# Adjacency tiles kept in bf16 in 32 buffers, layer 1's sums dealt anew to the steps, and a new order of the end

## The chip, the core and the metric

The kernel runs on one core of a Trainium2 chip. The metric is the device time of one execution in microseconds (us). Three runs of the kernel before took 260.06, 260.49 and 262.83 us, median 260.49. One more execution was profiled: 261.3 us, of which 259.5 us lie between its first and last instruction (the span). All times from a trace are counted from the span's start.

Engines: PE is TensorE (matrix products), DVE VectorE, ACT ScalarE, POOL GpSimd, SP SyncE. POOL and SP also issue transfers (DMA). Each engine works through its own queue in order; semaphores make one wait for another.

## The reference

Two layers of a graph network over N = 4096 nodes with 64 features; `adj` is 4096 x 4096 of zeros and ones, one in 256 is set.

```python
def layer0(x, adj, weight, bias):
    support = x @ weight
    mask = (adj != 0)
    rank = cumsum(mask, axis=1); deg = rank[:, -1:]
    k = minimum(deg, 100); pos = rank - (deg - k)
    w = mask * where(pos > 0, 0.5 ** (k - pos), 0)
    return w @ support + bias

def layer1(X, adj, W, b):
    deg = clip(sum(adj, axis=1) + 1, 1)
    h = (adj @ X + X) / deg
    z = relu(concat([X, h]) @ W + b)
    return z / maximum(norm(z), 1e-12)

x = layernorm(x + layer0(x, adj, weight, bias))
x = layernorm(x + layer1(x, adj, W, b))
```

Layer 0 weighs each neighbour by its rank counted from the row's end, so every row has to be counted from the right. Layer 1 needs layer 0's output for all neighbours. Both read the whole of `adj`.

## The kernel before

**Tiles.** The nodes (rows of `adj`, columns of its transpose) are cut into 8 slabs g of 512, the neighbours into 8 blocks k of 512 (each four times 128). A tile (g, k) of the transposed `adj` is read from HBM as float32 (1 MB) and written to SBUF as bf16 (512 KB) by a transfer that POOL issues (`load_next`, L106). There are 64 tiles, and 64 **steps**, one for each tile: slab by slab, in each slab from block 7 down to block 0. Step i handles tile i.

**A step** (loop from L542) does, on PE: `count` (column sums of tiles ahead, L247), `weigh` (ranks by two sets of 16 small products, L277 and L286), `some_sums` (a **group**, that is four products of layer 1's sum over one tile, L313), at the end of a chunk `spread` (L265), and `gather` (layer 0's sum with the weights of the step before, L304). ACT and DVE each turn half of the ranks into weights (L293, L294). The chunks are 1 to 4 tiles long (4 in slabs 4 to 7); the counts of the next chunk are made two tiles at a time in every second step, so step s of a pair counts tiles s+4 and s+5 where chunks are 4 long, and all of the next four in step 30. PE's queue is in order, so a count that waits for its tile's landing holds up all that follows.

**Loads.** Six are issued ahead; step i issues load i+6. The pool `a16` has 23 buffers; a load takes one that is free in program order or waits until its last reader is done. A tile's last reader is its group of layer 1's sum. For slabs 0 to 3, blocks 7 to 4, `keep_next` makes an fp8 copy of a tile (zeros and ones are exact in it) in two halves, one a step, three in four on ACT (L329) and the others on DVE (L327), so that the bf16 buffer comes free without a sum.

**Layer 1's sums.** A group (g, k) can only be summed when layer 0 is done for the nodes of block k, which is some steps after slab k's last step (`ready`: i >= 8(k+1) + 7, and tile (g, k) is there). `jobs` lists (slab, first block, end block); each job accumulates in one PSUM bank (`acc1`) and is then added to the slab's `part` by `evict_part`, on DVE. 27 of the 64 groups are done within the steps, 37 after them.

**Layer 0's epilogue** of slab g runs some steps later (`first_hT` ... `first_c1`, hung to steps by `at`): layer norm, the split of x1 into two fp16 halves (`x1hl`), and the products for layer 1 (`c1`).

**The end** (from L737): the last gather, slab 7's epilogue, the remaining groups (`own`, and `own_half` for slab 7 in two halves of its columns), and layer 1's epilogue by **units** of one or two slabs: `last_hT` (PSUM plus part to SBUF), `last_pz` (product with the neighbour weights), `last_z`, `last_sq`, `last_ss` (row norms), `last_rn` (1/sqrt by POOL's power or by a root of ACT and four steps of DVE), `last_y` (and the added x1, by POOL or DVE), `last_mv` (moments), `last_r`, `last_o`, `store`. The order is written by hand: units (5,2), (0,1), (4,3), 6, 7. Its tiles come from pools of two buffers each.

Of the kernel before, what the change touches and what calls it, by code (L numbers as in the profile page):

```python
# [12 lines left out]
F8 = mybir.dt.float8e4  # L13
# [23 lines left out]
KEPT = 4  # L37
# [3 lines left out]
def adj_resnorm_kernel(  # L41
# [31 lines left out]
    a16p = ctx.enter_context(tc.tile_pool(name="a16", bufs=23))  # L73
    a8p = ctx.enter_context(tc.tile_pool(name="a8", bufs=KEPT * (NK - KEPT)))
# [3 lines left out]
    small = ctx.enter_context(tc.tile_pool(name="small", bufs=2))  # L78
# [236 lines left out]

    to_keep = [(g, k, h) for g in range(KEPT) for k in range(NK - 1, KEPT - 1, -1) for h in range(2)]
    kept = {}

    def keep_next(i):
        if not to_keep:  # L320
            return
        g, k, h = to_keep.pop(0)
        if h == 0:
            kept[g, k] = a8p.tile([P, KB, R], F8, tag="a8", name=f"a8_{g}_{k}")
        qs = slice(h * KB // 2, (h + 1) * KB // 2)
        if i % 4 == 3:
            nc.vector.tensor_copy(kept[g, k][:, qs, :], A[g][k][:, qs, :], saturate=False)  # L327
        else:
            nc.scalar.copy(kept[g, k][:, qs, :], A[g][k][:, qs, :], saturate=False)  # L329
        if h == 1:  # L330
            A[g][k] = kept[g, k]


    jobs = [(0, 0, 2), (1, 0, 2), (2, 0, 2), (3, 0, 3), (2, 2, 4), (0, 2, 4), (1, 2, 4)]
    jobs += [(4, 0, 4), (5, 0, 5), (6, 0, 3)]
    have = {g: 0 for g in range(NG)}
    acc1 = {}

    todo = [(g, b, b == k0 * KB, b == k1 * KB - 1) for g, k0, k1 in jobs for b in range(k0 * KB, k1 * KB)]
# [5 lines left out]
    def evict_part(g):  # L345
        acc = acc1.pop(g)
        if g in part:
            nc.vector.tensor_tensor(part[g], acc, part[g], ALU.add)
        else:
            part[g] = const.tile([P, R], F32, name=f"part_{g}")  # L350
            nc.vector.tensor_copy(part[g], acc)

    def some_sums(i, n):

        done = None
        while n and todo and done is None and ready(i, todo[0][0], todo[0][1]):
            g, b, first, last = todo.pop(0)
            if first:
                acc1[g] = ps_a.tile([P, R], F32, tag="acc1", name=f"acc_part_{g}_{b}")
            second(acc1[g], g, b, first, last)  # L360
            have[g] = b // KB + 1
            n -= 1
            if last:
                done = g
        return done
# [176 lines left out]
    for c, chunk in enumerate(chunks):  # L542
# [7 lines left out]
        for (g, k), share in zip(chunk, shares):  # L550
# [25 lines left out]

            if i > NK and i % NK:
                keep_next(i)
# [7 lines left out]
            if done is not None:  # L586
                evict_part(done)
# [3 lines left out]
    L = NG - 1  # L591
    acc = {}
    a_half, b_half = slice(0, R // 2), slice(R // 2, R)

    def own(g, b0, b1):

        for b in range(b0, b1):
            second(acc[g], g, b, b == have[g] * KB, b == NB - 1)

    def own_half(rows, b0, b1):  # L600
        for b in range(b0, b1):
            nc.tensor.matmul(
                acc[L, rows.start],
                lhsT=x1hl[:, b, :],
                rhs=A[L][b // KB][:, b % KB, rows],
                start=b == 0,
                stop=b == NB - 1,
            )

    def last_hT(g):  # L610
        ep["hT", g] = epi.tile([P, R], F32, tag="hT", name=f"hT1_{g}")
        if g in part:
            nc.vector.tensor_tensor(ep["hT", g], acc[g], part[g], ALU.add)
        else:
            nc.scalar.copy(ep["hT", g], acc[g])

    def half_hT(rows):
        if rows.start == 0:
            ep["hT", L] = epi.tile([P, R], F32, tag="hT", name=f"hT1_{L}")
        nc.scalar.copy(ep["hT", L][:, rows], acc[L, rows.start])  # L620


    def unit(*slabs):
        return "_".join(map(str, slabs)), [g * TB + t for g in slabs for t in range(TB)]

    def half_unit(h):
        return f"{L}{'ab'[h]}", [L * TB + 2 * h, L * TB + 2 * h + 1]

    def spans(bs):

        for t in range(0, len(bs), TB):
            n = min(TB, len(bs) - t)
            yield slice(t, t + n), slice(bs[t], bs[t] + n)

    def last_pz(u):

        name, bs = u
# [5 lines left out]
    def last_z(u):  # L643

        name, bs = u
        z = ep["z", name] = epi.tile([P, len(bs), D], F32, tag="z", name=f"z_{name}")
# [3 lines left out]
    def last_sq(u, on_act):  # L650
        name, bs = u
        z = ep["z", name]
        sq = ep["sq", name] = epi.tile([P, len(bs), D], F32, tag="sq", name=f"sq_{name}")
        if on_act:
            nc.scalar.activation(sq, z, AF.Relu)  # L655
# [4 lines left out]
    def last_ss(u):  # L660
        name, bs = u
        ss = ep["ss", name] = small.tile([P, len(bs)], F32, tag="ss", name=f"ss_{name}")
        nc.vector.tensor_reduce(ss, ep["sq", name], AX.X, ALU.add)
# [3 lines left out]
    def last_rn(u, on_pool):  # L667
        name, bs = u
        ss = ep["ss", name]
        if on_pool:  # L670
            ep["rn", name] = root_p(ss, None, name, "rn")
        else:
            ep["rn", name] = root_b(root_a(ss, zero, f"n_{name}"), ss, zero, f"n_{name}")

    def last_y(u, on_pool, y=None):
        name, bs = u
        n = len(bs)
        if y is None:
            y = epi.tile([P, n, D], F32, tag="y", name=f"y1_{name}")
        ep["y1", name] = y  # L680
        rn = ep["rn", name].unsqueeze(2).to_broadcast([P, n, D])
        nc.vector.scalar_tensor_tensor(y, ep["z", name], 0.0, rn, ALU.max, ALU.mult)
        engine = nc.gpsimd if on_pool else nc.vector
# [3 lines left out]
    def last_mv(u, mv=None):  # L687
        name, bs = u
        ep["mv1", name] = moments(ep["y1", name], f"l1_{name}", mv)

    def last_s(u):
        name, bs = u
        ep["s1", name] = root_a(ep["mv1", name][:, :, 1], eps_ln, f"l1_{name}")

    def offset(u, engine):
        name, bs = u
        mv, r = ep["mv1", name], ep["r1", name]
        off = ep["off", name] = small.tile([P, len(bs)], F32, tag="off", name=f"off_{name}")
        if engine is nc.vector:
            engine.scalar_tensor_tensor(off, mv[:, :, 0], -1.0, r, ALU.mult, ALU.mult)  # L700
        else:
            engine.tensor_tensor(off, mv[:, :, 0], r, ALU.mult)
            engine.tensor_scalar(off, off, -1.0, None, ALU.mult)

    def last_r(u, on_pool):
        name, bs = u
        v = ep["mv1", name][:, :, 1]
        if on_pool:
            ep["r1", name] = root_p(v, LN_EPS, name, "r1")
            offset(u, nc.gpsimd)  # L710
        else:
            ep["r1", name] = root_b(ep["s1", name], v, eps_ln, f"l1_{name}")
            offset(u, nc.vector)

    def last_o(u, t0, t1, on_act=True):
        name, bs = u
        y, mv, r, off = ep["y1", name], ep["mv1", name], ep["r1", name], ep["off", name]
        if t0 == 0:
            ep["o", name] = wp.tile([P, len(bs), D], F32, tag="w", name=f"o_{name}")
        o = ep["o", name]  # L720
        for t in range(t0, t1):
            if on_act:
                nc.scalar.activation(
                    o[:, t, :], y[:, t, :], AF.Identity, bias=off[:, t : t + 1], scale=r[:, t : t + 1]
                )
            else:
                nc.vector.tensor_scalar(
# [3 lines left out]
    def store(u):  # L731
        name, bs = u
        for t, c in spans(bs):
            g, c0 = divmod(c.start, TB)
            nc.sync.dma_start(out=out[g][:, c0 : c0 + c.stop - c.start, :], in_=ep["o", name][:, t, :])

    gather(*held)  # L737
    run(NS, DVE)
    first_hT(L)
    va = ps_v.tile([P, 2, R], F32, tag="v", name="va")  # L740
    vb = ps_v.tile([P, 2, R], F32, tag="v", name="vb")

    def acc_of(g, tag, rows=R, name=None):
        return ps_a.tile([P, rows], F32, tag=tag, name=f"acc_right_{name or g}")

    acc.update({5: va[:, 0, :], 2: vb[:, 0, :], 1: va[:, 1, :], 4: vb[:, 1, :]})
    acc[0] = acc_of(0, "acc1")
    last = L * KB
    own(5, 20, 24)
    first_pz(L)  # L750
    first_y(L)
    first_mv(L)
    first_s(L)
    first_r(L)
    first_x1(L)
    first_hi(L)
    first_xl(L)
    first_lo(L)
    first_least(L)
    own(5, 24, last)  # L760
    own(2, 16, last)
    own(0, 16, 20)
    first_px(L)
    first_x1T(L)
    own(0, 20, 24)
    own(5, last, NB)
    last_hT(5)
    own(2, last, NB)
    last_hT(2)
    first_pu(L)  # L770
    first_c1(L)

    u = unit(5, 2)
    last_pz(u)
    own(0, 24, NB)
    last_z(u)
    last_sq(u, True)
    last_hT(0)
    last_ss(u)
    last_rn(u, True)  # L780
    own(1, 16, NB)
    last_hT(1)
    last_y(u, True)
    own(4, 16, 24)

    v = unit(0, 1)
    last_pz(v)
    own(4, 24, NB)
    last_mv(u)
    last_r(u, True)  # L790
    last_z(v)
    last_sq(v, True)
    last_hT(4)
    last_ss(v)
    last_rn(v, True)
    last_o(u, 0, 8)
    store(u)
    acc[3] = acc_of(3, "acc0")
    own(3, 12, NB)
    last_y(v, True)  # L800
    last_hT(3)
# [107 lines left out]
```

## Time and profile before

| what | value |
|---|---|
| median of three runs | 260.49 us |
| profiled execution | 261.3 us, span 259.5 us |
| PE, DVE, ACT, POOL busy | 218.3, 177.1, 147.6, 81.9 us |
| first and last weights on ACT (L293) | start 11.1 and 202.9 us |
| last output written by ACT (L723) | ends 256.1 us |
| transfers to SBUF | 37.38 MB, mean 144 GB/s |
| eviction to `part` on DVE (L351, L348) | 7 and 3 times, 0.68 us each |
| fp8 copies on ACT (L329), DVE (L327) | 23 of 1.04 us, 9 of 0.69 us |

How to read it: a line of the page or of a timeline names the source line, engine, operation, output and inputs. "Idle before" is the time in which the engine had nothing to do just before the instruction, and the name behind the arrow is what ended it. Matmuls are pipelined: the start of one group to the start of the next tells more than a duration. The granted clock is TensorE's, as a share of full speed.

### The profile page before, as it was taken

The page shows a single profiled execution, that of the slowest core. Times are in us where ns is not written, and L with a number is a line of the kernel's source. Part 1 is how long each engine was busy: PE and PEld are TensorE (multiplying, and loading weights), DVE is VectorE, ACT ScalarE, POOL GpSimd, SP SyncE. Part 2 cuts the span into 40 slices and gives each one's busy share as a digit, 9 for nine tenths or more (in the row PEclk, how much of TensorE's full clock was granted, in tenths as well). Part 3 has the DMA queues.
Part 4 walks back from the last instruction along what each step waited for, and adds up shares of the span by engine and source line. Part 5 has one row for each costly group of instructions (what it writes and reads, how often), then busy time and mean ns, then how long its engine had stood idle before and what let it go on. Part 6 is the DMA issues. An engine that isn't in the chain of part 4 may idle for free.

```text
span 259.5 us, 7477 instructions
## 1 busy us (share of the span) xinstructions
PE 218.3 (84%) x3202; PEld 100.1 (39%) x3202; DVE 177.1 (68%) x455; ACT 147.6 (57%) x210; POOL 81.9 (32%) x139
## 2 busy tenths in 40 slices
PE   7776778679979995999789799998996989999920
PEld 2222224224424431443344234433442636646910
DVE  5666767687797695557957594668577556555873
ACT  5376767587877676656866475447444421064271
POOL 8555695051013240230222322130200000475640
PEclk9999999999999999799999999999999999999975
DMA  5999999999999999599899999996400000000111
GB/s 105 192 233 245 242 214 215 224 213 215 221 214 189 205 186 214 93 168 215 167 151 178 201 214 213 222 203 131 104 0 3 3 0 3 0 30 11 43 40 42
DMA packets 11313, 37.38 MB, mean 144 GB/s; under 512 B 1424, under 2 KB 2576, under 8 KB 11280
## 3 DMA queue, kind: packets, MB, share of 16 engines
q0 software_dynamic: 9984, 35.66, 70.0%
q1 hardware_dynamic: 1296, 1.25, 1.4%
q8 instruction: 25, 0.41, 0.6%
q14 instruction: 8, 0.07, 0.1%
HBM read 69.40 MB, written 1.05 MB: 271 GB/s over the span
## 4 chain that ended last, share of the span: by engine, by line
PE 35%; DMA 26%; DVE 14%; issue 9%; POOL 7%; ACT 7%; POOLq 0%; ACTq 0%; DVEq 0%
DMA a<-in_adjT_dram 22%; PE acc L304 6%; PE acc_part L313 6%; ACT w L293 5%; PE v L277 4%; DMA c<-in_x_quads_dram 4%; PE acc_right L313 3%; DVE w L294 3%; PE v L286 3%; PE cnt L247 2%; POOL a L106 2%; DVE x L442 2%; PE pz L641 2%; PE va L313 2%; PE vb L313 2%
## 5 line engine op out<-in xcount | busy, mean ns | idle before, releaser
L293 ACT ACTIVATE w<-v,less 128x1024 int16<-128x1024 f32 x64 | 71.3, 1114 | 51.2 <-PE v L286 33.3
L294 DVE TENSOR_SCALAR w<-v 128x1024 int16<-128x1024 f32 x64 | 78.3, 1223 | 29.0 <-PE v L286 24.9
L106 POOL DMA_DIRECT2D a<-in_adjT_dram x64 | 37.0, 579 | 107.3 <-PE acc_part L313 41.5
L304 PE MATMUL acc<-w,xhl 128*128 128x512 bf16 x256 | 70.5, 384 | 0.2 <-ACT hT L409 0.2
L247 PE MATMUL cnt<-a,pick 128*32 128x512 bf16 x256 | 22.4, 386 | 18.3 <-DMA a<-in_adjT_dram 17.6
L277 PE MATMUL v<-a,tri 32*32 32x512 bf16 x1024 | 30.3, 386 | 7.1 <-ACT w L293 6.3
L304 PEld LDWEIGHTS <-xhl 128*128 128x128 f16 x256 | 22.3, 98 | 36.2 <-issue 15.0
L313 PEld LDWEIGHTS <-x1hl 128*128 128x128 f16 x224 | 19.6, 98 | 29.4 <-issue 10.6
L257 DVE TENSOR_TENSOR cs<-cnt,cs 128x512 bf16<-128x512 f32 x22 | 15.2, 690 | 22.9 <-PE cnt L247 22.9
L286 PE MATMUL v<-near,mine 32*32 32x512 bf16 x1024 | 29.3, 376 | 0.0
L313 PE MATMUL acc_part<-a,x1hl 128*128 128x512 bf16 x108 | 28.0, 382 | 0.0
L329 ACT CAST a<-a 128x1024 fp8e4<-128x1024 bf16 x23 | 23.9, 1038 | 0.0
L267 ACT ACTIVATE near<-rep,most 128x512 bf16<-128x512 f32 x30 | 20.5, 682 | 5.2 <-PE rep L265 5.2
L277 PEld LDWEIGHTS <-tri 32*32 32x32 bf16 x1024 | 11.5, 88 | 29.4 <-issue 27.4
L247 PEld LDWEIGHTS <-pick 128*32 128x32 bf16 x256 | 5.4, 93 | 32.8 <-issue 20.4
L393 POOL TENSOR_TENSOR rn<-ss,power 128x8 f32<-128x8 f32 (+1 forms) x4 | 6.0, 1506 | 34.8 <-DVE ss L665 34.7
L265 PE MATMUL rep<-cs,further 128*128 128x512 bf16 x30 | 11.6, 387 | 1.7 <-DVE cs L259 1.0
L313 PE MATMUL acc_right<-a,x1hl 128*128 128x512 fp8e4 (+1 forms) x56 | 12.9, 379 | 0.0
L655 ACT ACTIVATE sq<-z 128x512 f32<-128x512 f32 x3 | 1.9, 631 | 17.2 <-DVE z L648 17.2
L402 DVE BATCH_NORM_STATS2 st_l<-y 128x6 f32<-128x64 f32 x60 | 9.0, 213 | 1.0 <-POOL y L685 0.8
L237 POOL TENSOR_TENSOR x<-x,wts 128x256 f32<-128x256 f32 x8 | 5.8, 729 | 11.8 <-DMA x<-in_x_dram 11.7
L447 ACT CAST x1hl<-x 128x256 f16<-128x256 f32 x8 | 3.2, 405 | 10.8 <-DVE x L442 10.8
(134 smaller groups left out, 264.7 us busy)
## 6 DMA issues: line engine op xcount, KB each, us to landing
a<-in_adjT_dram POOLq DMA_DIRECT2D x64, 512.0 KB, 9.6
c<-in_x_quads_dram POOLq DMA_DIRECT2D x8, 128.0 KB, 11.7
x<-in_x_dram POOLq DMA_DIRECT2D x8, 128.0 KB, 9.1
out_dram<-o SPq DMA_DIRECT2D x8, 128.0 KB, 1.7
wts<-in_weights_dram SPq DMA_DIRECT2D x1, 192.0 KB, 7.2
```

Source lines behind the costliest of these rows:

```text
L106: nc.gpsimd.dma_start(out=a, in_=adjT[g, k])
L247: nc.tensor.matmul(cnt[g][quarters[q], :], lhsT=pick[:, PW - 4 * k : PW - 4 * k + Q], rhs=A[g][k][:, q, :], start=first, stop=last,)
L257: nc.vector.tensor_tensor(new, cnt[g], cs[g], ALU.add)
L265: nc.tensor.matmul(pr, lhsT=further, rhs=cs[g], start=True, stop=True)
L267: nc.scalar.activation(near[g], pr, AF.Relu, bias=most, scale=-1.0)
L277: nc.tensor.matmul(v[e // 2][quarters[q], e % 2, :], lhsT=tri[quarters[e], :], rhs=A[g][k][quarters[e], q, :], start=True, stop=False,)
L286: nc.tensor.matmul(v[e // 2][quarters[q], e % 2, :], lhsT=mine[quarters[e], 4 * k + q, :], rhs=nr[quarters[e], :], start=False, stop=True,)
L293: nc.scalar.activation(w[:, 0:2, :], v[0], AF.Relu, bias=less)
L294: nc.vector.tensor_scalar(w[:, 2:4, :], v[1], -STEP * MAX_NEIGH, 0.0, ALU.add, ALU.max)
L304: nc.tensor.matmul(acc0[g], lhsT=xhl[:, b, :], rhs=w[:, q, :].bitcast(BF16), start=(k, q) == (NK - 1, 0), stop=(k, q) == (0, KB - 1),)
L313: nc.tensor.matmul(acc, lhsT=x1hl[:, b, :], rhs=A[g][b // KB][:, b % KB, :], start=first, stop=last)
L329: nc.scalar.copy(kept[g, k][:, qs, :], A[g][k][:, qs, :], saturate=False)
```

## The change

The fp8 copies (`keep_next`) and their pool go; `a16` has 32 buffers instead of 23 plus 16 of half the size. `jobs` now lists blocks one by one and deals 39 groups to the steps, 25 to the end. A finished job is evicted before the step's gather instead of at the step's end, and a slab's first eviction is a copy on ACT. The end takes its work tiles (`hT`, z, squares, y, outputs) from `a16`, uses five or six PSUM banks as they come free, has units (0,1), (4,5), 2, 3, 6 and 7 in halves, and a new order of all its calls.

```diff
-    a16p = ctx.enter_context(tc.tile_pool(name="a16", bufs=23))
-    a8p = ctx.enter_context(tc.tile_pool(name="a8", bufs=KEPT * (NK - KEPT)))
+    a16p = ctx.enter_context(tc.tile_pool(name="a16", bufs=32))
-    small = ctx.enter_context(tc.tile_pool(name="small", bufs=2))
+    small = ctx.enter_context(tc.tile_pool(name="small", bufs=4))
...
-    to_keep = [(g, k, h) for g in range(KEPT) for k in range(NK - 1, KEPT - 1, -1) for h in range(2)]
-    def keep_next(i):
...
-    jobs = [(0, 0, 2), (1, 0, 2), (2, 0, 2), (3, 0, 3), (2, 2, 4), (0, 2, 4), (1, 2, 4)]
-    jobs += [(4, 0, 4), (5, 0, 5), (6, 0, 3)]
+    jobs = [(0, [0]), (1, [0])]
+    jobs += [(2, [0, 1]), (0, [1]), (1, [1])]
+    jobs += [(3, [1, 0, 2]), (0, [2]), (1, [2]), (2, [2]), (4, [2, 1, 0, 3])]
+    jobs += [(0, [3]), (1, [3]), (2, [3]), (5, [3, 2, 1, 0, 4]), (3, [3, 4])]
+    jobs += [(6, [4, 3, 2, 1, 0, 5]), (4, [4, 5]), (0, [4, 5]), (1, [4, 5]), (2, [4])]
...
             part[g] = const.tile([P, R], F32, name=f"part_{g}")
-            nc.vector.tensor_copy(part[g], acc)
+            nc.scalar.copy(part[g], acc)
...
-            if i > NK and i % NK:
-                keep_next(i)
+            if done is not None:
+                evict_part(done)
             if held is not None:
                 gather(*held, half)
             held = (g, k, w)
             if g > 0 and k == NK - 1:
                 first_hT(g - 1)
             run(i, PE)
             run(i, DVE)
-            if done is not None:
-                evict_part(done)
...
+    banks = [va[:, 0, :], vb[:, 0, :], va[:, 1, :], vb[:, 1, :], ps_a.tile([P, R], F32, tag="acc1", name="va1")]
+    def own(g, k):
+        if g not in acc:
+            acc[g] = bank()
+        for b in range(k * KB, (k + 1) * KB):
+            count_of[g] += 1
+            second(acc[g], g, b, count_of[g] == 1, count_of[g] == len(left[g]) * KB)
...
+    def hT_of(g):
+        j = g // 2
+        if j not in hTs:
+            hTs[j] = a16p.tile([P, 2, R], F32, tag="a16", name=f"hT1_{j}")
+        return hTs[j][:, g % 2, :]
...
+    def last_relu(u):
+        nc.scalar.activation(u[2][1], u[2][0], AF.Relu)
```

The head, middle and tail of the new order of the end, with lines left out:

```python
    own_half(1, 2)
    first_hT(L)
    own(5, 6)
    first_pz(L)
    own(2, 5)
...
    own(0, 7)
    own(1, 7)
    last_hT(0)
    own(5, 7)
    last_hT(1)
    own(4, 7)
    last_hT(5)
    u01 = unit(0, 1)
    last_pz(u01)
    last_hT(4)
    u45 = unit(4, 5)
    last_pz(u45)
    last_z(u01)
...
    last_r(u7)
    store(u3)
    last_add(u6)
    offset(u7)
    last_mv(u6)
    last_o(u7, 0, 2, nc.scalar)
    last_o(u7, 2, 4, nc.vector)
    last_r(u6)
    store(u7)
    offset(u6)
    last_o(u6, 0, 4)
    store(u6)
```

## The prediction

> **What bounds the kernel now.** I read the page first (rows 2 and 5), then the load's line, the TensorE (PE) and GpSimd (POOL) timelines around one pair of steps, and the busy time of chosen stretches. Times are of the profiled execution: 261.3 us, of which the span is 259.5; it ran 0.8 above the median of the three runs, 260.49.
>
> From the page, the granted clock by fortieth of the span, and the line of adj's loads (busy, mean ns, then idle before and who ended it):
>
> ```profile
> PEclk9999999999999999799999999999999999999975
> L106 POOL DMA_DIRECT2D a<-in_adjT_dram x64 | 37.0, 579 | 107.3 <-PE acc_part L313 41.5
> ```
>
> POOL's queue stood 107 us in front of loads, and layer 1's sums (acc_part) ended most of that: a load waits until its buffer has been used up. The load's own line adds the time from issue to landing:
>
> ```profile
> DMA to landing us min/median/max: 5.0/9.6/17.3
> ```
>
> The PE timeline; in brackets, idle time and what ended it. First the count of step 12, then of step 30, then steps 40 and 41, then the counts of step 58 and the start of the end:
>
> ```profile
> 49.35 0.40 PE L247 MATMUL cnt<-a,pick 128*32 128x512 bf16 x4 [2.08 <-DMA a<-in_adjT_dram]
> ...
> 102.70 0.40 PE L247 MATMUL cnt<-a,pick 128*32 128x512 bf16 x4 [2.02 <-DMA a<-in_adjT_dram]
> ...
> 134.11 0.40 PE L247 MATMUL cnt<-a,pick 128*32 128x512 bf16 x4 [0.47 <-DMA a<-in_adjT_dram]
> 134.44 0.43 PE L277 MATMUL v<-a,tri 32*32 32x512 bf16 x16
> 134.67 0.42 PE L286 MATMUL v<-near,mine 32*32 32x512 bf16 x16
> 135.03 1.04 PE L313 MATMUL acc_part<-a,x1hl 128*128 128x512 bf16 x4
> 135.90 1.03 PE L304 MATMUL acc<-w,xhl 128*128 128x512 bf16 x4
> 136.86 0.43 PE L277 MATMUL v<-a,tri 32*32 32x512 bf16 x16
> ...
> 189.62 0.62 PE L247 MATMUL cnt<-a,pick 128*32 128x512 bf16 x8
> ...
> 205.19 1.03 PE L313 MATMUL va<-a,x1hl 128*128 128x512 bf16 x4
> ```
>
> And POOL's timeline at those steps:
>
> ```profile
> 128.98 0.57 POOL L106 DMA_DIRECT2D a<-in_adjT_dram  x1 [4.46 <-ACT a L329]
> ...
> 136.36 0.53 POOL L106 DMA_DIRECT2D a<-in_adjT_dram  x1 [2.57 <-PE acc_part L313]
> ```
>
> The issue at 128.98 is load 45 (slab 5, block 2); step 40 counts it at 134.11, 5.13 us later, with PE waiting. The sums that end at 136.07 (135.03 + 1.04) release the next issue at 136.36, 0.29 later. Stretches, columns as on the page (length; PE, PEld, DVE, ACT, POOL busy; clock; DMA share; GB/s): the gated window after step 30's wait, a stretch of late steps, and the end up to the last output:
>
> ```profile
> 103.40:106.80 3.40, 3.40 (x57) 1.28 (x41) 1.90 (x4) 2.65 (x4) 0.00 (x0) 0.50 0.57 114
> 160.00:172.00 12.00, 12.00 (x194) 5.18 (x197) 7.59 (x17) 5.88 (x7) 2.89 (x5) 1.00 1.06 218
> 205.20:256.10 50.90, 41.73 (x274) 26.55 (x272) 31.41 (x145) 17.86 (x46) 18.85 (x25) 0.94 0.06 19
> ```
>
> So steps up to 30 follow the loads, those near 160 to 172 are full on PE, and the end is PE for 43 us and then a VectorE/ScalarE (DVE/ACT) chain.
>
> **Unit costs on PE**, from the starts in its timeline: a step's weights 0.59, a group of sums 0.87, a gather 0.96, two tiles' counts 0.54, a spread 0.21; per slab pz 1.01, px 0.3, pu 0.87. Eight steps with eight groups: 4x0.54 + 8x2.42 + 2x0.21 + 2.18 = 24.1 us, 3.0 a step, 2.15 without a group.
>
> **Part 1, loads up to step 38.** With 32 buffers the first 32 loads wait for none and the next six for sums of step 26 or earlier; before, waiting began with load 23. Unhindered, the page shows some 215 GB/s: 524 KB in 2.44 us, 2.52 with each slab's x. Step 30 counts load 35; from load 15, counted at 49.35, that is 20 x 2.52 = 50.4, so 99.75 instead of 102.70. Then PE carries seven groups in eight steps, 24.1 - 0.87 = 23.2, to step 38's last count at 122.9 (before: 127.3). Gain 4.4.
>
> **Part 2, loads 44 to 63: a new wait.** The dealing frees no tile early. At step i load i+6 needs i-25 spent tiles, and from step 38 to 57 exactly that many groups are done; in the built program each of these loads waits for the sums of the step just before it. Step s counts tile s+5 (s even), which is released by the sums of step s-2. Before, these releases lay 2.5 to 5 steps ahead (load 53: step 44 for step 48). So a pair of steps becomes a loop: last count to end of sums 1.96 (134.11 to 136.07), sums to issue 0.29, issue to landing. The landing is what I can't read directly: 5.13 with little queued, 9.2 at the worst (138.78 to 147.95, behind a slab of x and two loads). Here the load ahead was issued about 5 us earlier and is nearly in, so I take 5.25 and keep both ends: pair 7.4 to 11.4, taken 7.5. Behind the blocked count in PE's queue stand the weights, sums and gather of the step; ACT and DVE wait for them. Ten pairs, step 38 to 58: 75.0 against 189.9 - 127.3 = 62.6 now. Loss 12.4.
>
> What PE has to do between release and count is 3.4 us without a slab's epilogue, so in five of ten pairs it idles about 2.0. The row at 103.40 shows what that can cost: after waits of 0.72 and 2.02 within 99.5 to 103.4 the clock was granted at 0.50 for 3.4 us, 1.7 us of work lost, while 1.78 at 147.95 lost none. I count 0.6 of one such window over the ten pairs, +1.0, since 2.0 lies between the row that lost and the one that did not; ends 0 and 5 x 1.7 = 8.5.
>
> [...]
>
> **Part 3, steps 58 to 63** get groups that they lack now: 6 x 0.87 = 5.2. Part of this fills waits for evictions (now 189.9 to 205.2 is 15.3). PE's own list is 0.33 + 6x2.42 + 0.21 + 0.96 + 1.2 = 17.2, so +1.9.
>
> **Edits at nothing within the steps.** The 32 fp8 half copies go: 23 on ACT (23.9 us), 9 on DVE (6.2). ACT was 49% and DVE 63% busy in 160 to 172, and before step 30 loads decide; what the copies delayed is in Part 1. Evictions grow from 10 to 20, 7 of them on ACT (0.59, the slab copies' row), 13 on DVE at 0.68. DVE's weights began at 161.43 and end at 162.65; an eviction ends at 163.33, the next sums began at 163.57. If that cover of 0.24 fails by 0.2 each, it is 4 us. Sums from bf16 instead of fp8 tiles: 379 ns for both. SP's stores and their sizes stay.
>
> **Part 4, the end.** Twelve groups fewer: 48 x 0.216 = 10.4 of PE's 41.7. But DVE then binds. Slab 7's chain (hT copy to low half) took 205.2 to 212.3, covered by 8.4 us of older groups, so the first layer-1 hT can start 9.3 after the stretch begins. DVE's work from there: hT 4.8, z 3.2, sums of squares 4.5, y 3.1, moments 7.7, c1 0.85, the halves' small steps and the last outputs 3.0: 27.2 (a 27.5 us DVE load stands from 214.5 to 255.8 now). Walking the new order with POOL's rows (power 1.67 for 8 values, adds 1.41 for two slabs, both in one queue), DVE waits some 4.2 for POOL, mostly for the first adds and slabs 2 and 3: 40.7. Slab 6 is stored last: POOL's root 1.3 and four ACT outputs of 0.36 more: 43.5 instead of 50.9, -7.4. Bounds: no wait at all 39.3 (-11.6); as much idle on DVE as now, 41.3 - 27.5 = 13.8, gives 53 (+2). The last store's 3.4 us stay.
>
> **Sum:** -4.4 + 12.4 + 1.0 + 1.9 - 7.4 = +3.5. That is 264.8 for the profiled execution, 264.0 for the median.
>
> **Rivals.** (A) Faster: the new wait is hidden. Place: count of tile s+5; it decides when a load lands within PE's 3.4 to 5.4 us between release and count. Then pairs cost 60.3 and the sum is -4.4 - 2.3 + 1.9 - 7.4 = -12.2: 248.3. For it: 5.0 is a minimum that includes other traffic. Against: no load of 64 beat 5.0, and half the pairs offer 3.4. (B) The clock halves after every long wait: 7.5 more, 271.5. For it the row at 103.40, against it 147.95. (C) The end's new order brings nothing, because DVE waits for POOL as now: 271.4. For it: POOL's 18.9 us of slow small steps stay; against: the adds of one unit now lie beside another unit's DVE work.
>
> **Numbers.** Forecast 0.57 (own range 260 to 268), A 0.16, B 0.12, C 0.15. Most of A (0.13) and half of B and C lie outside 256 to 271. A measurement here tells about 1% (257.9 to 263.1) from no change: faster 0.17 (A and a sliver of the forecast), same 0.21 (the forecast's lower third), slower 0.62. Predicted 264.0.
>
> **What would show it.** Loads 32 to 37 issued without waiting; step 30's last count near 100; from step 40 to 58 counts idle 1 to 2 us, ended by DMA, one pair every 7.5 us; POOL's loads then all released by acc_part of the step before; the stretch from the last gather to the last output near 43.5 with DVE its busiest engine after PE. Wrong if pairs stay near 6, if PEclk shows several dips, or if the end is as long as now.

## The result, and the profile after

| | before | after |
|---|---|---|
| median | 260.28 us (4 runs, 260.06 to 262.83) | 270.76 us (4 runs, 269.63 to 276.29) |
| ratio | | 1.0365, 95% interval 1.027 to 1.0459: slower |
| profiled execution, its span | 261.3, 259.5 | 271.59, 269.8 |

The run of 276.29 was a disturbed one; the ratio leaves it out. The forecast was 264.0, with 260 to 268 as its own range and 256 to 271 as the wide one. The sign was right, but the time lies above the first range and just inside the second, and the change is about three times the 3.5 us of the sum. Where the 10.3 us of the two profiled spans came from, stage by stage (all points read in the two timelines; "weights" is the start of a step's first half of the weights on ACT):

| stage | before | after | difference | forecast |
|---|---|---|---|---|
| start to weights of step 38 | 128.9 | 125.5 | -3.4 | -4.4 |
| weights of step 38 to those of step 58 | 62.1 | 75.6 | +13.6 | +12.4 and +1.0 |
| from there to the end of the last gather | 14.2 | 16.85 | +2.65 | +1.9 |
| the end: last gather to last output | 50.9 | 45.8 | -5.1 | -7.4 |
| last output to the span's end | 3.43 | 5.94 | +2.5 | 0 |

The first lines to read are those of the page of after that answer to those shown of before: the granted clock by fortieth of the span, and two groups (busy time and mean ns of one; then idle time of the engine before them and what ended most of it).

```profile
PEclk9999999799999999999999999979999999999755
...
L103 POOL DMA_DIRECT2D a<-in_adjT_dram x64 | 35.1, 550 | 110.4 <-PE acc_part L310 60.2
L244 PE MATMUL cnt<-a,pick 128*32 128x512 bf16 x256 | 23.0, 387 | 23.4 <-DMA a<-in_adjT_dram 22.5
```

Before's line for the second group was:

```profile
L247 PE MATMUL cnt<-a,pick 128*32 128x512 bf16 x256 | 22.4, 386 | 18.3 <-DMA a<-in_adjT_dram 17.6
```

POOL still stands about as long in front of loads (110.4 us, before 107.3), but more of it is ended by layer 1's sums: 60.2 instead of 41.5. PE's idle time ahead of counts grew from 18.3 to 23.4 us although the first half of the steps waits less. There are now two dips of the clock in the steps instead of one, in the eighth and in the twenty-seventh slice.

The wait itself is seen in after's PE timeline over one pair of steps (start, duration, engine, line, operation; in brackets the idle time and what ended it; x3 where one of a group's four products is missing from the records):

```profile
146.84 0.40 PE L244 MATMUL cnt<-a,pick 128*32 128x512 bf16 x4 [1.72 <-DMA a<-in_adjT_dram]
147.76 1.04 PE L310 MATMUL acc_part<-a,x1hl 128*128 128x512 bf16 x3
...
152.00 0.40 PE L244 MATMUL cnt<-a,pick 128*32 128x512 bf16 x4
154.13 0.40 PE L244 MATMUL cnt<-a,pick 128*32 128x512 bf16 x4 [1.73 <-DMA a<-in_adjT_dram]
```

And in POOL's timeline at the same place:

```profile
149.09 0.53 POOL L103 DMA_DIRECT2D a<-in_adjT_dram  x1 [4.34 <-PE acc_part L310]
```

This is the loop that the prediction described. A count gets its tile at 146.84; the sums behind it in PE's queue end at 147.76 + 1.04 = 148.80; that frees a buffer, and POOL issues the load 0.29 us later; it lands 5.04 us after that, at 154.13, and PE has stood still for 1.73 us. From count to count it is 7.29 us.

The stretch of steps 38 to 58 as a whole, in before and then in after (length; PE, PEld, DVE, ACT, POOL busy with the number of instructions; clock; DMA share; GB/s):

```profile
128.90:191.00 62.10, 58.59 (x961) 25.75 (x960) 41.43 (x83) 33.88 (x43) 14.66 (x25) 1.00 0.88 169
```

```profile
125.50:201.10 75.60, 62.33 (x959) 27.66 (x972) 39.87 (x80) 32.35 (x40) 13.89 (x25) 0.98 0.79 145
```

PE has nearly the same number of instructions to run in both (961 and 959). Before, it was busy 58.6 of 62.1 us, so it was the bound; after, 62.3 of 75.6, and the transfers move less in a microsecond (145 GB/s for 169). Neither engine nor transfers are full any more: they wait for each other in turn, which is what a loop through a buffer's release looks like.

### The profile page after: what moved, and what is told of

Same layout as the page of the kernel before. It is cut to its first block, busy times and chain, and to the rows that moved or that the text cites. A ratio compares the mean times of both kernels' runs of the same rounds, so it can differ in the third digit from the quotient of the medians.

```text
span 269.8 us, 7424 instructions
## 1 busy us (share of the span) xinstructions
PE 214.4 (79%) x3162; PEld 99.9 (37%) x3202; DVE 172.9 (64%) x441; ACT 132.1 (49%) x197; POOL 83.3 (31%) x146
## 4 chain that ended last, share of the span: by engine, by line
DMA 42%; PE 27%; issue 11%; POOL 10%; DVE 4%; ACT 2%; POOLq 0%; ACTq 0%; DVEq 0%
DMA a<-in_adjT_dram 33%; PE acc_part L310 7%; PE acc L301 5%; DMA x<-in_x_dram 5%; DMA c<-in_x_quads_dram 4%; PE v L274 3%; PE va L310 3%; POOL a L103 2%; POOL r L374 2%; PE v L283 2%; PE vb L310 2%; PE cnt L244 2%; PE pz L653 2%; POOL x L234 1%; ACT u L739 1%
## 5 line engine op out<-in xcount | busy, mean ns | idle before, releaser
L301 PE MATMUL acc<-w,xhl 128*128 128x512 bf16 x239 | 67.4, 387 | 2.5 <-issue 1.3
L103 POOL DMA_DIRECT2D a<-in_adjT_dram x64 | 35.1, 550 | 110.4 <-PE acc_part L310 60.2
L244 PE MATMUL cnt<-a,pick 128*32 128x512 bf16 x256 | 23.0, 387 | 23.4 <-DMA a<-in_adjT_dram 22.5
L310 PE MATMUL acc_part<-a,x1hl 128*128 128x512 bf16 x137 | 37.7, 387 | 2.7 <-issue 2.4
L301 PEld LDWEIGHTS <-xhl 128*128 128x128 f16 x256 | 23.5, 99 | 35.2 <-issue 11.4
L283 PE MATMUL v<-near,mine 32*32 32x512 bf16 x1024 | 28.9, 382 | 0.0
L244 PEld LDWEIGHTS <-pick 128*32 128x32 bf16 x256 | 5.9, 93 | 39.3 <-issue 26.5
L274 PEld LDWEIGHTS <-tri 32*32 32x32 bf16 x1024 | 10.2, 88 | 24.9 <-issue 23.5
L374 POOL TENSOR_TENSOR rn<-ss,power 128x4 f32<-128x4 f32 (+1 forms) x5 | 6.4, 1280 | 34.1 <-DVE ss L676 33.9
L739 ACT ACTIVATE u<-u,off,r 128x64 f32<-128x64 f32 x28 | 9.8, 427 | 5.0 <-POOL off L732 5.0
L310 PE MATMUL va<-a,x1hl 128*128 128x512 bf16 x38 | 9.3, 379 | 0.1
L283 PEld LDWEIGHTS <-mine 32*32 32x32 bf16 x1024 | 9.1, 88 | 0.3 <-issue 0.3
L330 DVE TENSOR_TENSOR part<-acc_part,part 128x512 f32<-128x512 f32 x13 | 8.8, 681 | 0.0
```

The source lines that it names most:

```text
L103: nc.gpsimd.dma_start(out=a, in_=adjT[g, k])
L244: nc.tensor.matmul(cnt[g][quarters[q], :], lhsT=pick[:, PW - 4 * k : PW - 4 * k + Q], rhs=A[g][k][:, q, :], start=first, stop=last,)
L274: nc.tensor.matmul(v[e // 2][quarters[q], e % 2, :], lhsT=tri[quarters[e], :], rhs=A[g][k][quarters[e], q, :], start=True, stop=False,)
L283: nc.tensor.matmul(v[e // 2][quarters[q], e % 2, :], lhsT=mine[quarters[e], 4 * k + q, :], rhs=nr[quarters[e], :], start=False, stop=True,)
L301: nc.tensor.matmul(acc0[g], lhsT=xhl[:, b, :], rhs=w[:, q, :].bitcast(BF16), start=(k, q) == (NK - 1, 0), stop=(k, q) == (0, KB - 1),)
L310: nc.tensor.matmul(acc, lhsT=x1hl[:, b, :], rhs=A[g][b // KB][:, b % KB, :], start=first, stop=last)
```

## The experiments

Theory T: the loss sits in steps 38 to 58 and is the loop sums, issue, landing, count, because 32 buffers let a load be released just one pair of steps ahead of its count. Rivals: R1, the seven evictions moved to ACT, and all evictions moved ahead of the gather, hold up the steps; R2, PE is simply full there with the groups that the change adds. For the end and what follows it: D, POOL's closing drain has become the last thing; P and others are named where they come up.

**One more buffer, and the room for it by itself.** A pool of 33 buffers releases every load one step earlier. The room comes from five changed lines (tiles of z with one buffer, three lines of which one is shown, one start tile in cs's buffer and t1 in y's); the control has these with 32 buffers.

```diff
-    a16p = ctx.enter_context(tc.tile_pool(name="a16", bufs=32))
+    a16p = ctx.enter_context(tc.tile_pool(name="a16", bufs=33))
-    of_m = epi.tile([P, P], I32, tag="z", name="of_m")
+    of_m = epi.tile([P, P], I32, tag="z", bufs=1, name="of_m")
-    has = epi.tile([P, P], BF16, tag="sq", name="has")
+    has = one.tile([P, P], BF16, tag="cs", name="has")
...
-        t1 = epi.tile([P, TB, D], F32, tag="sq", name=f"t1_{g}")
+        t1 = epi.tile([P, TB, D], F32, tag="y", name=f"t1_{g}")
```

> One more bf16 buffer (33), nothing else that matters to the order; its room comes from a single buffer for z, t1 in y's buffers and two start tiles in cs's. From step 38 on each load then waits for the sums of two steps before instead of one. Theory T (the loop release, landing, count): from step 38 to 58 a pair of steps takes 6.0 to 6.4 us instead of the changed kernel's 7.57 (75.7 for ten), the idle time before counts that DMA ended falls by 10 or more, and the time is 256 to 260 us instead of 270.8. Rival R1 (the ten more evictions, now ahead of the gather, hold up PE) and rival R2 (PE is simply full with ten more groups): pairs stay at 7.4 or more and the time at 268 to 272.

> The room that the 33rd buffer takes is made in the same way (z's single buffer, t1 and two start tiles elsewhere), but the buffers stay 32. All theories: as the changed kernel, 269 to 272 us, pairs 7.4 to 7.7. If it is faster or slower by 2 or more, the other run with 33 has to be read against this one.

Measured: 33 buffers 259.35 us (10 runs), 0.9942 of before (0.991 to 0.9973); the control 271.03 (one run). Steps 38 to 58 took 62.7 us with 33 buffers, 74.9 in the control and 75.6 in after. The PE timeline of the version with 33 buffers, and then its POOL timeline:

```profile
140.58 1.04 PE L310 MATMUL acc_part<-a,x1hl 128*128 128x512 bf16 x4
142.41 0.61 PE L244 MATMUL cnt<-a,pick 128*32 128x512 bf16 x8
143.54 1.04 PE L310 MATMUL acc_part<-a,x1hl 128*128 128x512 bf16 x3
...
147.78 0.62 PE L244 MATMUL cnt<-a,pick 128*32 128x512 bf16 x8
```

```profile
141.91 0.53 POOL L103 DMA_DIRECT2D a<-in_adjT_dram  x1 [2.10 <-PE acc_part L310]
```

The counts at 147.78, two tiles in one row, have no bracket: they waited for nothing. The load of the second tile was released by the sums that end at 141.62, one step earlier than in after, and issued at 141.91. PE came to the row 5.87 us later, and the load, whose own four products are the second half of the row, did not hold it up; the loads that after's counts wait for land in 5.0 to 5.4. The loop is the same; it only has one more step's work inside it. Of the ten waits with 11.6 us in all, one of 0.8 is left. This settles the cause of the loss in these steps: neither the evictions (R1) nor PE's work (R2) changed, the control kept the loss, and with the 33rd buffer it went.

**The sums ahead in the step.** The other way to lengthen the loop is to let the sums, which release the buffer, run before the count that waits.

```diff
+            n_todo = len(todo)
+            done = some_sums(i, QUOTA)
+            if done is not None:
+                evict_part(done)
...
-            n_todo = len(todo)
-            done = some_sums(i, QUOTA)
...
-            if done is not None:
-                evict_part(done)
```

> The step's sums and their eviction stand ahead of the step's counts and weights instead of behind them; as many buffers, groups and evictions as in the changed kernel. The sums of a step no longer stand behind the counts that wait for a load. T: the sums of step s release their buffer before PE waits for step s's counts, the loop spans two pairs, and a pair of steps 38 to 58 takes 6.0 to 6.5 us; 256 to 260 us. R1 and R2: as many evictions and groups, so pairs stay near 7.5 and the time at 268 to 272.

Measured: 262.64 us (10 runs), 1.0094 of before (1.0049 to 1.0139), steps 38 to 58 67.1 us. So most of the loss went, as T says, but 5.0 us of it stayed, more than expected. In its PE timeline four waits for loads are left with 4.6 us; one of them, and the issue of that load in POOL's timeline:

```profile
152.03 0.40 PE L244 MATMUL cnt<-a,pick 128*32 128x512 bf16 x4 [0.82 <-DMA a<-in_adjT_dram]
```

```profile
146.79 0.53 POOL L103 DMA_DIRECT2D a<-in_adjT_dram  x1 [2.87 <-PE v L283]
```

This load was issued not 0.3 us after the sums, which ended at 145.52 (144.48 + 1.04), but 1.27 us after them, and the trace names the rank products (L283) as what released it. From issue to count it took 5.24 us, as in after. The kernel says why the release is late: `ready` lets a group be summed in the very step in which its tile is ranked. With the sums moved ahead, the last reader of such a tile is no longer its group of sums but its rank products. By `jobs` this holds for 15 groups, and the summary of this run's loads (idle time before them, and how often) has as many:

```profile
  PE v L283: 48.4, 15
```

The four loads that are waited for (the 45th, 51st, 53rd and 59th, counted from 0) all take the buffer of such a group. No run tested this further.

**The evictions as they were.** R1 by itself: all evictions at the step's end and on DVE.

```diff
-            nc.scalar.copy(part[g], acc)
+            nc.vector.tensor_copy(part[g], acc)
...
-            if done is not None:
-                evict_part(done)
             if held is not None:
...
+            if done is not None:
+                evict_part(done)
```

> The evictions go back to the step's end and all to VectorE, as before the change; deal, buffers and end stay changed. T: pairs of steps 38 to 58 stay at 7.4 to 7.7 and the time at 269 to 273. R1: pairs fall to 6.5 or less and the time below 264. R2: unchanged.

Measured: 271.76 us (one run; three of after's were 269.63 to 271.59), steps 38 to 58 73.5 us. Of the 2.1 us less, up to 1.7 are the dip of the clock that after had there (half speed for 3.41 us) and this execution had not (mean clock 0.963, after's 0.955). The ten waits for loads shrank to 8.0 us, and 2.7 us of waits for evictions came in their place: a step made longer in another way only fills the loop's slack. R1 falls.

**The drain.** After the last output, the span of after runs on for 5.94 us, before's for 3.43. The last rows of before's timeline for POOL and ACT:

```profile
250.72 0.45 POOL L685 TENSOR_TENSOR y<-y,x 128x128 f32<-128x128 f32 x1
...
255.33 0.77 ACT L723 ACTIVATE o<-y,off,r_l 128x64 f32<-128x64 f32 x2 [1.22 <-DVE off L700]
```

and those of after:

```profile
262.14 0.23 POOL L732 TENSOR_SCALAR off<-off 128x4 f32<-128x4 f32 x1
262.41 1.43 ACT L739 ACTIVATE u<-u,off,r 128x64 f32<-128x64 f32 x4 [2.15 <-POOL off L732]
```

In before POOL's last work ended at 251.17, five microseconds ahead of the last output; in after at 262.38, and the last output waits for it. The trace also records each engine's closing drain: POOL's ends at 257.79 in before and at 269.00 in after, 6.6 us behind its last work in both. SP, which issues the stores, passes its own last wait at 258.35 in before, later than POOL's drain; in after at 266.08, and the program then waits 2.9 us more for POOL. Two experiments test this from both sides. The first adds one small POOL operation (0.22 us) that nothing needs late in before's end:

```diff
+    late = small.tile([P, TB], F32, tag="late", name="late")
+    nc.gpsimd.tensor_scalar(late, ep["off", w[0]], -1.0, None, ALU.mult)
```

> In the kernel before the change one small POOL instruction is added that reads the last offset, which VectorE writes at 255.2 of 259.5 us; nothing waits for it. Theory D: POOL's drain then ends some 6.6 after 255.5, near 262, and the time grows by 3 to 4 us, to 263.5 to 264.5. Rival (the stores decide the end): no change, 260 to 261.

Measured: 264.23 us (4 runs; before in the same series 260.87), 1.0117 of before (1.005 to 1.0184); last output to the span's end 7.10 us for 3.43. Its row in POOL's timeline:

```profile
253.84 0.22 POOL L868 TENSOR_SCALAR late<-off 128x4 f32<-128x4 f32 x1 [4.09 <-DVE off L700]
```

It ends at 254.06 and the span at 261.8, 7.7 us later; in after the span ends 7.4 us behind POOL's last work. An operation of 0.22 us on an idle engine made the kernel 3.4 us longer.

The second takes POOL's root out of the last slab of after, by one line that makes ACT and DVE do it:

```diff
     last_mv(u6)
+    last_s(u6)
```

> In the changed kernel slab 6's last 1/sqrt and offset move from POOL to ACT's root and VectorE's four steps, so POOL's last work is the add of slab 6, which ended at 258.8 of 269.8 us. Theory D (POOL's drain at the program's end takes some 6.6 us from POOL's last work, whatever else is done: 251.18 to 257.79 before the change, 262.38 to 269.00 after it): the drain ends near 265.3 and no longer decides, from the last output to the end takes 3.4 instead of 5.9, and the chain loses another 0.8: 3 to 3.5 us faster, 267.3 to 268. Rival (the last store lands late because two stores follow each other): the distance from the last output to the end stays near 5.9 and the gain is 0.8 to 1.

Measured: last output to the span's end 3.36 us, the end itself 45.1, both as expected, but the median of 4 runs was 270.5 (267.49 to 272.99), 1.0325 of before (1.0249 to 1.0401) where after had 1.0365: the gain of 3.3 did not show in the time. In the profiled execution the steps had taken 2.8 us longer than in after, with three dips of the clock (0.953 in the mean, 0.955 in after). The waits of after's steps make such a difference from run to run likely, but one profile does not show it. So the line was tried again where the steps do not wait:

**Both remedies together**, 33 buffers and the root of slab 6 on ACT and DVE.

> 33 buffers (in the room found before) and slab 6's last root on ACT and DVE instead of POOL. Theory (the wait of loads and POOL's late drain are two separate costs of the change, which add): the version with 33 buffers alone took 259.35; the root moved takes 2.6 us off the time between last output and end (5.94 to about 3.4) and 0.7 off the end itself, so about 256 (255 to 257), ratio to before about 0.983. Rival (the drain is hidden by something else, or the root's gain is eaten by the steps): 258.5 to 260, with the time from last output to end still near 5.9 or the steps longer.

Measured: 255.95 us (6 runs), 0.9826 of before (0.979 to 0.9861), last output to the span's end 3.51, the end 45.1. Against 259.35 that is 3.4 less, the 3.3 expected; by the two ratios to before, each from its own series, it is 3.0. The two costs are separate, and the drain's is shown. This version beats both kernels.

**What made the end 2.3 us longer than forecast.** Two candidates in the trace of after were tried. PE idles 1.7 us ahead of slab 7's product pz_7a, which waits for a copy on ACT that stands behind eight outputs of unit 01 (P); and DVE waits for POOL's additions (D). On top of the version just shown, first the copy, and the products that it needs, ahead of four of those outputs:

```diff
+    own_half(0, 6)
+    half_hT(0)
     last_o(u01, 0, 2)
     last_add(u2)
     last_z(u7b)
     last_o(u01, 4, 6)
-    own_half(0, 6)
...
-    half_hT(0)
```

> The same, with slab 7's first hT copy (and the four products that it waits for) ahead of unit 01's last four outputs on ACT, where PE idles 1.7 us in front of pz_7a for it. Theory P (PE's wait for that copy is what makes the end 2.3 us longer than forecast): the end from last gather to last output falls from about 45.1 to 43.5 to 44. Theory D (DVE is what binds there, and it waits for POOL's adds of slabs 2 and 3; pz_7a is needed only after that): pz_7a starts about 1.2 us earlier, the end stays at 45.1 within 0.3.

Measured: the end 45.1 as without it, 256.66 us (4 runs, 0.9847 with 0.98 to 0.9895). The whole timeline of this version, DVE and PE rows:

```profile
234.61 0.66 PE L653 MATMUL pz_7a<-wts,hT 128*128 128x64 f32 x4 [0.46 <-ACT hT L621]
...
235.55 0.60 DVE L383 BATCH_NORM_STATS2 st_l<-u 128x6 f32<-128x64 f32 x4 [1.40 <-POOL u L699]
```

The product came earlier by the 1.24 us that PE's wait lost (0.46 for 1.70), but DVE still waits 1.40 us for POOL and reaches what depends on pz_7a no sooner. P falls. Then instead the additions for slabs 2 and 3 on DVE:

```diff
-        engine = nc.vector if ("sn", name) in ep else nc.gpsimd
+        engine = nc.vector if ("sn", name) in ep or name in "23" else nc.gpsimd
```

> The same as the first of these three, with the additions of x1 for slabs 2 and 3 on DVE (0.41 each) instead of POOL (0.72 each). Theory D: DVE's two waits for POOL there (1.40 and 0.96 us) go and two operations of 0.41 come, POOL's queue gets 1.45 shorter: the end falls by 1 to 2 us, from about 45.1 to 43.1 to 44.1, and the time to about 254.5. Theory P: no change, or 0.8 us more for the DVE work added.

Measured: the end 43.8 us, 254.98 us (6 runs), 0.9799 of before (0.9763 to 0.9836). The two waits for POOL (1.40 and 0.96) are gone, and this came up in DVE's timeline:

```profile
237.33 0.29 DVE L659 TENSOR_TENSOR u<-pz_7a,c 128x128 f32<-128x128 f32 x1 [0.89 <-PE pz_7a L653]
```

D holds as what binds there, with 1.3 us in the profiled end; the medians differ by 1.0, and their intervals overlap. It does not show where the 2.3 came from: the forecast had already counted waits for POOL (see the account of the end below). Now pz_7a was late, so the two edits were made together.

> Both edits of the end: the additions for slabs 2 and 3 on DVE, and slab 7's first hT copy ahead of the last four outputs of unit 01. Theory (waits of one engine cover one another: the early copy brought nothing while DVE waited for POOL, but with the additions on DVE the trace shows DVE waiting 0.89 us for pz_7a, which waits for that copy): the end falls by 0.6 to 0.9 us from 43.8, to 42.9 to 43.2, and the time from 254.98 to about 254.2. Rival (DVE's own work is what is left, and POOL's roots come late instead): the end stays at 43.8 within 0.2, with a new wait of DVE or ACT in place of the 0.89.

Measured: the end 43.9 us, 254.9 us (6 runs), 0.9788 of before (0.9759 to 0.9818): no different from the additions alone. The wait of 0.89 went, and DVE's timeline has two others in its place:

```profile
237.33 0.43 DVE L693 SCALAR_TENSOR_TENSOR u<-u,rn 128x256 f32<-128x256 f32 x1 [0.61 <-POOL rn L374]
...
241.83 0.42 DVE L674 TENSOR_REDUCE ss<-u 128x4 f32<-128x256 f32 x1 [0.21 <-ACT u L667]
```

The rival held: behind the wait that was removed stood POOL's root for slab 3.

## Why the prediction was right or wrong

**The new wait: right, in mechanism and size.** A pair of steps was forecast at 7.5 us with a landing of 5.25; it took 7.56 (75.6 over ten pairs) with landings of 5.0 to 5.4. The forecast's 12.4 for the wait and 1.0 for the clock make 13.4; 13.6 was measured, and 33 buffers, which alter only the release, take 12.9 of it away (75.6 to 62.7). One detail was off: I had PE idle about 2.0 us in five of the ten pairs. All ten waited, 11.6 us together: four without work of a slab's epilogue 1.41 to 1.90, and six 0.50 to 1.07, since the epilogue is split over two pairs of each slab (px and pu in one, pz in the next). And one reading was: layer 1's sums ended 41.5 of the 107.3 us in which POOL stood in front of loads, the largest share but not most; nothing was worked out from it. Rival A (the wait is hidden, 248.3) failed at its own point of decision: the landings never came below the 5.0 that the 64 loads of before had shown, and PE's work in the loop was less than that in every pair. With one step more in the loop, it was hidden.

**The clock: right, by luck of the phase.** One gated window came in steps 38 to 58, where 0.6 were counted. The two waits of 1.72 and 1.73 us above cost none; behind this one the clock was at one half from 177.23 for 3.41 us:

```profile
176.62 0.40 PE L244 MATMUL cnt<-a,pick 128*32 128x512 bf16 x4 [1.90 <-DMA a<-in_adjT_dram]
```

Rival B (a window after every long wait, 271.5) gave nearly the time that was measured, but not by its mechanism: it asked for several dips and there was one. The same wait of 2.08 us early in the steps (ending at 49.35 before, at 49.44 after) was followed by no dip in before and by one at 50.93 in after. So the length of one wait does not decide. What does was not settled by a run; the two traces show this. The clock's changes are whole multiples of a dip's length, 3.413 us, apart: in after 126.30 from dip to dip in the steps (37 times) and 75.09 from there to the drop at 252.32 in the end (22 times), in before 146.77 from the dip to the drop at 250.16 (43 times). Cut into windows of that length counted from a dip, PE's time without a product fills 0.61 and 0.56 of the window just ahead of after's two dips, and from 8 us to the last gather at most 0.41 of any other. In before it fills 0.68 ahead of the one dip (at 103.39) and at most 0.53 elsewhere, because a window's end at 48.77 cuts the wait of 2.08 in two. By these two traces it counts how much of a wait falls into one window, and counted from the span's start the windows begin at 0.99 us in before and at 3.15 in after; that is the luck. But 0.53 without a dip and 0.56 with one lie close together, and no run moved a wait to test this reading.

**Part 1 (-4.4, measured -3.4): the size was off.** Step 30's last count came at 100.53 instead of 99.75, and its own first wait for the loads 0.1 later than before's; the 20 loads between took 51.1 us, 2.55 each instead of 2.52. The rest came from step 30 to 38, for which seven groups had been counted at PE's price alone; PE also waited there 0.35 and 0.23 us for ACT's weights.

**Part 3 (+1.9, measured +2.65)** was mis-sized by 0.75. The sum took PE's own list of work, without a wait. In after's trace PE waits once in this stretch for the weights of ACT, longer than the miss; no run tested what this wait is worth:

```profile
211.45 0.44 PE L274 MATMUL v<-a,tri 32*32 32x512 bf16 x16 [1.08 <-ACT w L290]
```

**The edits at nothing: right.** Undoing the evictions' new place and engine brought no time back (271.76, one run), so the cover of 0.24 us did not have to bear anything: the wait for loads lay over it.

**The end (-7.4, measured -5.1): the step that failed is "DVE waits some 4.2 for POOL".** The other terms held within 0.7: the first hT of layer 1 started 9.4 us after the last gather (9.3 forecast), and from there DVE had 26.5 us of work (27.2 forecast, with a few operations that lie before) until slab 7's last output; slab 6's rest was 3.2 (2.8). What was left is read from the stretch between, in after (columns as above):

```profile
218.00:263.84 45.84, 31.01 (x223) 22.14 (x224) 30.44 (x137) 18.90 (x49) 22.33 (x32) 0.87 0.06 21
227.41:260.60 33.19, 21.65 (x167) 16.70 (x167) 26.46 (x115) 15.76 (x41) 20.80 (x29) 0.88 0.07 24
```

In the second row DVE is busy 26.46 of 33.19 us, so it was idle 6.7 instead of 4.2. Its timeline names whom it waited for:

```profile
230.00 1.29 DVE L616 TENSOR_TENSOR hT<-vb,part 128x512 f32<-128x512 f32 x2 [1.03 <-PE vb L310]
231.73 0.69 DVE L659 TENSOR_TENSOR u<-pz,c 128x512 f32<-128x512 f32 x1 [0.44 <-PE pz L653]
233.51 0.69 DVE L659 TENSOR_TENSOR u<-pz,c 128x512 f32<-128x512 f32 x1 [1.10 <-PE pz L653]
236.79 0.69 DVE L693 SCALAR_TENSOR_TENSOR u<-u,rn 128x512 f32<-128x512 f32 x1 [0.34 <-POOL rn L374]
...
248.79 0.61 DVE L383 BATCH_NORM_STATS2 st_l<-u 128x6 f32<-128x64 f32 x4 [1.40 <-POOL u L699]
...
252.72 0.60 DVE L383 BATCH_NORM_STATS2 st_l<-u 128x6 f32<-128x64 f32 x4 [0.96 <-POOL u L699]
```

For POOL it was 2.7 us (0.34 + 1.40 + 0.96), less than forecast. Forgotten were the waits for PE when the first units start (1.03, 0.44 and 1.10, and two more of 0.17 and 0.43, together 3.2): the walk through the order had taken PE's sums and products as being there. These waits stand unchanged in the traces of all versions of the end, and no run took them away: that they are what the forecast lacked is read from the trace, not tested. Rival C (no gain, DVE waits as before) was wrong.

**"The last store's 3.4 us stay": wrong, +2.5.** The sentence took the stretch from last output to end as a property of the store. In before the store did decide it, but narrowly: SP passed its last wait at 258.35, 0.6 us after the end of POOL's drain. The new order put slab 6's root on POOL into the last 3.5 us before the last output, and then POOL's closing drain, which ends 6.6 us after its last work, decides. Nothing in the trace's own chain of waits says so; it is seen by setting the end of each engine's last work beside the span's end. In the sum, the two misses at the end (2.3 and 2.5) and that of Part 1 (1.0) and Part 3 (0.75) make, with the 0.2 of the wait, the 6.8 us between the 264.8 that the sum gave for the profiled execution and its 271.59.

## What to carry to other kernels

When a change sets a number of buffers, follow one buffer round: last reader, issue, landing, first use; here the loop cost its length where the work between release and use was shorter than a landing (5.0 to 5.4 us), and one buffer more (12.9 us for 512 KB) took nearly the whole wait away. Moving the releasing sums ahead of the waiting count took 8.5 us of it; moving the evictions, next to nothing. A small operation that POOL had late set the program's end after all outputs were written (0.22 us cost 3.4); move such operations off POOL or to an earlier place. In a tail with three engines in turn, take the next wait behind the one that you remove as its price: here two waits of 2.4 us, removed for 0.8 us more of DVE's own work, gave 1.3, and the third edit gave nothing.

## What the runs showed that was not expected

- POOL's closing drain ends 6.62 us after POOL's last work in before and in after; DVE's and ACT's drains end less than 0.1 us after theirs (after: ACT's last output ends at 263.84, its drain at 263.88). What lies between the last output and the span's end goes with how far ahead of that output POOL's last work ended: 4.9 us ahead in before, 3.43 behind the output; 4.3 ahead in the version with both remedies (246.73 and 251.06), 3.51; 1.5 ahead in after, 5.94; 0.6 ahead with the added operation, 7.10.
- The loads that after's ten counts wait for, most of them issued 4.4 to 4.9 us behind the one ahead, take 5.0 to 5.4 us to land, although twenty loads on end came in every 2.55 us. With 33 buffers the loads follow each other more closely (in the POOL timelines, between 129 and 152 us, issues 2.4 to 3.9 us apart, in after 2.4 to 4.9), and PE waited for them but once (0.81 us). So what decides here is how early a load is released.
- In after's end, small operations of DVE were drawn out while POOL added beside them, but not beside its powers. From the timeline:

```profile
240.30 1.26 POOL L699 TENSOR_TENSOR u<-u,x 128x512 f32<-128x512 f32 x1 [0.70 <-DVE u L693]
240.52 1.07 DVE L676 TENSOR_TENSOR ss<-ss,least 128x4 f32<-128x4 f32 x1
```

The maximum of 128 x 4 (L676) took 1.07 us and ends with POOL's addition, at 241.59 and 241.56; another took 0.46 beside an addition of 0.45 (from 255.87), and the one at 245.35, with no addition beside it, 0.20. A step of a root (L361), 0.22 elsewhere, took 0.78 beside an addition of 0.72. Two maxima of 128 x 2 that started at 251.21 and 251.60, beside POOL's power of 250.96 to 252.00, took 0.16 each, as the two in before's end did. What makes the difference was not shown.
